# Weight tiles for field-pair products: a ring of three tiles loaded twelve pairs ahead, in place of two tiles loaded six pairs ahead

## The chip, the cores and the metric

The kernel runs on one core of one Trainium2 chip. The core has a tensor engine (PE; its weight loads are listed as PEld), a vector engine (DVE), a scalar engine (ACT), a GpSimd engine (POOL), a sync engine (SP) and 16 DMA engines that move data between HBM and the on-chip memory SBUF. The metric is the device time of one execution in microseconds (us). Before the change the median of six runs is 760.24 us (759.88 to 760.63).

## The reference

There are 32 fields. The input `r_inputs` has, for each of 1024 rows of the batch, one vector of 128 numbers per field. `W` holds one 128 by 128 matrix for each of the 496 pairs of fields i < j. For every pair the vector of field i is multiplied by the pair's matrix, and the result is multiplied element by element with the vector of field j:

```python
v_i = inputs[:, I_IDX, :]
v_j = inputs[:, J_IDX, :]
transformed = jnp.einsum('bpd,ped->bpe', v_i, W)
return transformed * v_j
```

All numbers are float32. The output has 1024 x 496 x 128 numbers, 260 MB; the weights are 32.5 MB and the fields 16.8 MB. The profile counts 49.28 MB read from HBM and 260.05 MB written.

## The kernel before

**Order of the pairs.** `_pairs()` walks i from 30 down to 0 and, for each i, j from i+1 to 31. Row i thus has 31-i pairs; the rows grow longer, and field 0, as the last i, is needed only for the last 31 pairs (465 to 495). It is never a j. A pair is done in two halves of 512 rows of the batch; the loop variable `u` counts halves and `q = u // 2` counts pairs. The batch lies along the free dimension, so a field is a tile of 128 partitions by 1024 numbers (4 KB in a partition, 512 KB in all).

**Loads.** `load_x(f)` loads one field, from SP before the loop and from ACT's queue inside it: at the first pair of row i it loads field i-7. Each field has a tile of its own that stays for the whole kernel (pool `x`). `load_w(c)` loads a weight tile: the matrices of eight pairs (`WL = 8`), 4 KB in a partition, 512 KB. Weight tiles come from a ring of `WB` = 2 buffers (pool `wr`). The first two are loaded before the loop by SP; the dictionary `w_at` says at which pair the others are issued, on ACT's queue (line 194): tile c at pair 8c-11, or later where the tile that held the buffer is still read by matmuls on unsplit weights (tile 2 at pair 8, tile 3 at pair 16).

**Splitting.** The first five rows (15 pairs, `nq0`) are multiplied as they are (line 159). For all others float32 is split into two shorter parts, and a product takes three matmuls. `split_w(c)` splits the weights of two pairs: ACT makes `wh` (line 95), POOL makes `wl` and `wd` (lines 96 to 98). It is taken from the list `todo` from pair 2c-5 on, so the first split of weight tile c comes six pairs after the tile's load was issued. `split_x(f, a)` does the same for half a field (lines 110 to 112, and `xd` on POOL at line 116 or, for the first ten split fields, on DVE at line 203). One item of `todo` is taken per pair.

**A half pair.** `first(u)` issues the matmuls of `wh` and `wl` (line 162), and ACT scales their sum in PSUM (line 163). `second(u)`, three halves later, adds the matmul of `wd` (line 171), and DVE multiplies PSUM by field j into the output tile `ot` (line 177). Three pairs share an `ot` of 1.5 MB, and SP writes it out when it is full (line 184); the first group and the last four pairs go out in smaller pieces. There are four `ot` buffers, so DVE can begin a group only when the write of the group four before it has landed.

**What sets the order.** The schedule is the program's order (`tc.manual_schedule()`): on each engine instructions run in the order in which the loop issues them, and a waiting instruction holds up all that is behind it on its engine. ACT's queue thus carries the issues of weight and field loads, the `wh` and `xh` splits and the scaling of every half pair; POOL's carries the rest of the splits; SP's carries the writes. A DMA is also issued only after the earlier DMA on the same completion semaphore has landed.

Of the kernel before, what the change touches and what calls it, by code (L numbers as in the profile page):

```python
# [7 lines left out]
F32 = mybir.dt.float32  # L8
# [3 lines left out]
P = 128  # L12
NF = 32
NQ = NF * (NF - 1) // 2
BT = 1024
HB = 512
WC = 2
WL = 8
# [3 lines left out]
SHARED = 10  # L22
XDLAG = 10
LAG = 3
WB = 2
WLEAD = 6
XLEAD = 5


# [6 lines left out]
def kernel(  # L36
# [22 lines left out]
    nc = tc.nc  # L59
# [3 lines left out]
    xpool = ctx.enter_context(tc.tile_pool(name="x", bufs=1))  # L63
    spool = ctx.enter_context(tc.tile_pool(name="xs", bufs=2))
    rpool = ctx.enter_context(tc.tile_pool(name="wr", bufs=WB))
    wpool = ctx.enter_context(tc.tile_pool(name="ws", bufs=4))
# [4 lines left out]

    def load_x(f, n=1, pieces=1, eng=None):

        t = xpool.tile([P, n, BT], F32, tag=f"x{f}", name=f"x_{f}")
        s = BT // pieces
        for k in range(pieces):
            (eng or nc.sync).dma_start(out=t[:, :, k * s : (k + 1) * s], in_=xt[:, f : f + n, k * s : (k + 1) * s])
        for k in range(n):
            x_sb[f + k] = t[:, k, :]
# [3 lines left out]
    def load_w(c, splits=(0, WL), eng=nc.scalar):  # L83
        w_raw[c] = rpool.tile([P, WL, P], F32, tag="w", name=f"w_{c}")
        for a, b in zip(splits, splits[1:]):
            eng.dma_start(out=w_raw[c][:, a:b, :], in_=wt[c, :, a:b, :])
# [44 lines left out]

    load_w(0, (0, 1, WL), nc.sync)
    load_x(NF - 2, pieces=2, eng=nc.scalar)
    load_x(NF - 1, pieces=2, eng=nc.scalar)
    load_x(NF - 3)
    load_x(NF - 4)
    load_w(1, eng=nc.sync)
    for f in range(NF - 5, NF - 4 - XLEAD, -1):
        load_x(f)


    w_at = {}
    for c in range(WB, -(-NQ // WL)):
        free = (c - WB + 1) * WL if (c - WB) * WL < nq0 else 0
        w_at[max(c * WL - 3 * WC + 1 - WLEAD, free)] = c


    ctx.enter_context(tc.manual_schedule())
# [3 lines left out]
    def first(u):  # L152
        q, h = divmod(u, 2)
        i, c = pairs[q][0], q // WC
        r = slice(q % WC * P, (q % WC + 1) * P)
        s = slice(h * HB, (h + 1) * HB)
        po[u] = ppool.tile([P, HB], F32, tag="po", name=f"po_{u}")
        if q < nq0:
            nc.tensor.matmul(po[u], w_raw[q // WL][:, q % WL, :], x_sb[i][:, s], start=True, stop=True)  # L159
        else:  # L160
            for t in (0, 1):
                nc.tensor.matmul(po[u], w_s[c][t][:, r], x_s[i][t][:, s], start=t == 0, stop=t == 1)  # L162
            nc.scalar.mul(po[u], po[u], 1.0 + EPS)  # L163

    def second(u):
        q, h = divmod(u, 2)
        i, j = pairs[q]
        r = slice(q % WC * P, (q % WC + 1) * P)
        s = slice(h * HB, (h + 1) * HB)
        if q >= nq0:  # L170
            nc.tensor.matmul(  # L171
                po[u], w_s[q // WC][2][:, r], x_s[i][2][:, s], start=False, stop=True, skip_group_check=True
            )
        g, k = divmod(q, OG)
        if k == 0 and h == 0:
            ots[g] = opool.tile([P, OG, BT], F32, tag="ot", name=f"ot_{g}")
        nc.vector.tensor_tensor(ots[g][:, k, s], po.pop(u), x_sb[j][:, s], ALU.mult)  # L177
        if q >= NQ - 2:
            nc.sync.dma_start(out=out[g, :, k, s], in_=ots[g][:, k, s])
        elif g == 0 or q >= NQ - 1 - OG:  # L180
            if h == 1:
                nc.sync.dma_start(out=out[g, :, k], in_=ots[g][:, k])
        elif k == OG - 1 and h == 1:
            nc.sync.dma_start(out=out[g], in_=ots[g])

    for u in range(2 * NQ + LAG):
        q = u // 2
        if u < 2 * NQ:
            i, j = pairs[q]
            if u % 2 == 0 and j == i + 1 and 0 <= i - 2 - XLEAD:  # L190
                load_x(i - 2 - XLEAD, eng=nc.scalar)
            first(u)
            if u % 2 == 1 and q in w_at:
                load_w(w_at[q])
        if u >= LAG:
            second(u - LAG)
        if u % 2 == 1:
            ready = [t for t in todo if t[0] <= q]
            if ready:
                ready[0][2](u)  # L200
                todo.remove(ready[0])
        while later and later[0][0] <= u:
            nc.vector.tensor_tensor(*later.pop(0)[1:], ALU.subtract)  # L203
# [28 lines left out]
```

## Time and profile before

The profiled execution took 759.89 us by its own time, 0.35 us under the median of the six runs; its span, from the first to the last instruction, is 758.0 us, so 1.89 us lie around it.

| | busy us | share of the span |
|---|---|---|
| PE matmul | 707.4 | 93% |
| DVE | 629.1 | 83% |
| ACT | 625.4 | 83% |
| POOL | 597.0 | 79% |
| DMA, 310.07 MB in 758 us | mean 409 GB/s | |

| transfer | count | size KB | median us from issue to landing |
|---|---|---|---|
| `ot` to HBM | 163 | 1536 | 13.5 |
| weight tile, from ACT | 60 | 512 | 9.0 |
| field, from ACT | 24 | 512 | 9.0 |
| field, from SP | 6 | 512 | 8.5 |

Busy time is a union of intervals, and matmuls overlap, so PE's 93% is not 93% of what PE could do. In the tables of stretches each row has a time window in us, the busy time of each engine with the count of its instructions, the granted clock of PE, the mean share of time in which the 16 DMA engines had a packet, and the rate. A DMA engine's packets overlap by some nanoseconds, so a share of 1.00 to 1.02 means that all 16 were occupied. In lists of waits a row reads: engine and line that waited, what it waited for, the sum in us, how often, the longest.

### The profile page before, as it was taken

The page shows a single profiled execution, that of the slowest core. Times are in us where ns is not written, and L with a number is a line of the kernel's source. Part 1 is how long each engine was busy: PE and PEld are TensorE (multiplying, and loading weights), DVE is VectorE, ACT ScalarE, POOL GpSimd, SP SyncE. Part 2 cuts the span into 40 slices and gives each one's busy share as a digit, 9 for nine tenths or more (in the row PEclk, how much of TensorE's full clock was granted, in tenths as well). Part 3 has the DMA queues.
Part 4 walks back from the last instruction along what each step waited for, and adds up shares of the span by engine and source line. Part 5 has one row for each costly group of instructions (what it writes and reads, how often), then busy time and mean ns, then how long its engine had stood idle before and what let it go on. Part 6 is the DMA issues. An engine that isn't in the chain of part 4 may idle for free.

```text
span 758.0 us, 11264 instructions
## 1 busy us (share of the span) xinstructions
PE 707.4 (93%) x2946; PEld 549.5 (72%) x2946; DVE 629.1 (83%) x1012; ACT 625.4 (83%) x1256; POOL 597.0 (79%) x863
## 2 busy tenths in 40 slices
PE   7979999999999999999998999999999999999992
PEld 3557778777777777777787777778787777777771
DVE  4869989997888879788797888888888888888883
ACT  1368889988888888888887978889899898989881
POOL 0959999999888987977878787888887878786650
PEclk9999999999999999999999999999999999999996
DMA  9999999999999999999999999999999999999996
GB/s 349 426 409 380 425 414 421 424 426 425 424 425 422 426 422 399 424 418 407 407 404 423 414 420 417 396 419 410 409 412 410 409 420 406 403 417 415 419 407 256
DMA packets 38800, 310.07 MB, mean 409 GB/s; under 512 B 4304, under 2 KB 4432, under 8 KB 17872
## 3 DMA queue, kind: packets, MB, share of 16 engines
q1 hardware_dynamic: 26064, 264.25, 83.2%
q10 hardware_dynamic: 12672, 45.09, 16.0%
q8 instruction: 24, 0.39, 0.2%
q14 instruction: 40, 0.33, 0.1%
HBM read 49.28 MB, written 260.05 MB: 408 GB/s over the span
## 4 chain that ended last, share of the span: by engine, by line
DMA 53%; PE 20%; DVE 19%; POOL 3%; issue 2%; ACT 1%; DVEq 0%; ACTq 0%; SPq 0%; POOLq 0%
DMA out_dram<-ot 50%; DVE ot L177 18%; PE po L162 13%; PE po L171 7%; DMA x<-in_xt_dram 2%; POOL xl L111 1%; DMA w<-in_wt_dram 1%; DVE xd L203 1%; POOL xl L112 1%; POOL xd L116 1%; POOL wl L96 0%; POOL wd L98 0%; ACT po L163 0%; DVEq L177 0%; POOL wd L97 0%
## 5 line engine op out<-in xcount | busy, mean ns | idle before, releaser
L177 DVE TENSOR_TENSOR ot<-po,x 128x512 f32<-128x512 f32 x992 | 614.9, 682 | 113.3 <-DMA out_dram<-ot 46.4
L163 ACT ACTIVATE po<-po 128x512 f32<-128x512 f32 x962 | 540.4, 582 | 58.6 <-PE po L162 23.0
L162 PE MATMUL po<-xh,wh 128*128 128x512 f32 x962 | 381.8, 397 | 12.8 <-DVE ot L177 11.9
L171 PE MATMUL po<-xd,wd 128*128 128x512 f32 x962 | 377.1, 392 | 13.7 <-ACT po L163 11.4
L162 PE MATMUL po<-xl,wl 128*128 128x512 f32 x962 | 378.2, 393 | 5.4 <-POOL wl L96 5.3
L96 POOL TENSOR_TENSOR wl<-w,wh 128x256 fp32r<-128x256 f32 x241 | 182.3, 756 | 74.1 <-ACT wh L95 63.6
L162 PEld LDWEIGHTS po<-xh,wh 128*128 128x128 f32 x962 | 181.2, 188 | 70.9 <-DVE ot L177 33.0
L171 PEld LDWEIGHTS po<-xd,wd 128*128 128x128 f32 x962 | 181.3, 188 | 56.5 <-issue 6.3
L162 PEld LDWEIGHTS po<-xl,wl 128*128 128x128 f32 x962 | 181.4, 189 | 46.2 <-POOL wl L96 10.2
L98 POOL TENSOR_TENSOR wd<-wl,wd 128x256 fp32r<-128x256 f32 x241 | 179.2, 743 | 20.1
L95 ACT ACTIVATE wh<-w 128x256 fp32r<-128x256 f32 x241 | 99.8, 414 | 42.1 <-DMA w<-in_wt_dram 36.6
L97 POOL TENSOR_SCALAR wd<-wh 128x256 fp32r<-128x256 f32 x241 | 98.8, 410 | 20.3
L111 POOL TENSOR_TENSOR xl<-x,xh 128x512 fp32r<-128x512 f32 x52 | 69.3, 1333 | 18.5 <-ACT xh L110 18.0
L116 POOL TENSOR_TENSOR xd<-xh,xl 128x512 fp32r<-128x512 f32 x32 | 41.4, 1292 | 2.7
L110 ACT ACTIVATE xh<-x 128x512 fp32r<-128x512 f32 x52 | 32.5, 629 | 12.6 <-DMA x<-in_xt_dram 12.6
L112 POOL TENSOR_SCALAR xl<-xl 128x512 fp32r<-128x512 f32 x52 | 33.3, 641 | 4.6
L159 PE MATMUL po<-x,w 128*128 128x512 f32 x60 | 28.4, 636 | 4.4 <-DMA x<-in_xt_dram 4.4
L159 PEld LDWEIGHTS po<-x,w 128*128 128x128 f32 x60 | 11.8, 202 | 20.2 <-issue 13.0
L203 DVE TENSOR_TENSOR xd<-xh,xl 128x512 fp32r<-128x512 f32 x20 | 17.1, 854 | 3.6 <-POOL xl L112 3.6
L110 ACT ACT_TABLE_LOAD x1 | 1.3, 1283 | 4.5 <-DMA w<-in_wt_dram 4.5
L219 POOL MEMSET const-float32-0.0<- 128x1 f32 x1 | 0.1, 99 | 0.2 <-issue 0.2
L219 POOL MEMSET const-bfloat16-1.0<- 128x1 bf16 x1 | 0.1, 102 | 0.0
(2 smaller groups left out, 0.2 us busy)
## 6 DMA issues: line engine op xcount, KB each, us to landing
out_dram<-ot SPq DMA_DIRECT2D x163, 1536.0 KB, 13.5
w<-in_wt_dram ACTq DMA_DIRECT2D x60, 512.0 KB, 9.0
x<-in_xt_dram ACTq DMA_DIRECT2D x24, 512.0 KB, 9.0
x<-in_xt_dram SPq DMA_DIRECT2D x6, 512.0 KB, 8.5
out_dram<-ot SPq DMA_DIRECT2D x5, 512.0 KB, 10.8
x<-in_xt_dram ACTq DMA_DIRECT2D x4, 256.0 KB, 5.8
out_dram<-ot SPq DMA_DIRECT2D x4, 256.0 KB, 10.1
w<-in_wt_dram SPq DMA_DIRECT2D x1, 512.0 KB, 8.1
```

Of the source, the lines that this page charges most:

```text
L95: nc.scalar.mul(h, raw, 1.0 - 2.0**-13)
L96: nc.gpsimd.tensor_tensor(l, raw, h.bitcast(F32), ALU.subtract)
L97: nc.gpsimd.tensor_scalar(d, h.bitcast(F32), EPS, 1.0, ALU.mult, ALU.mult)
L98: nc.gpsimd.tensor_tensor(d, l.bitcast(F32), d.bitcast(F32), ALU.subtract)
L111: nc.gpsimd.tensor_tensor(l, x_sb[f][:, s], h.bitcast(F32), ALU.subtract)
L112: nc.gpsimd.tensor_scalar(l, l.bitcast(F32), 1.0 / EPS, 1.0, ALU.mult, ALU.mult)
L116: nc.gpsimd.tensor_tensor(d, h.bitcast(F32), l.bitcast(F32), ALU.subtract)
L159: nc.tensor.matmul(po[u], w_raw[q // WL][:, q % WL, :], x_sb[i][:, s], start=True, stop=True)
L162: nc.tensor.matmul(po[u], w_s[c][t][:, r], x_s[i][t][:, s], start=t == 0, stop=t == 1)
L163: nc.scalar.mul(po[u], po[u], 1.0 + EPS)
L171: nc.tensor.matmul(po[u], w_s[q // WC][2][:, r], x_s[i][2][:, s], start=False, stop=True, skip_group_check=True)
L177: nc.vector.tensor_tensor(ots[g][:, k, s], po.pop(u), x_sb[j][:, s], ALU.mult)
```

## The change

The ring of weight tiles gets a third buffer (`WB` 2 to 3), and a weight tile is issued six pairs earlier (8c-17 in place of 8c-11). The third tile, number 2, is loaded by SP before the loop; in the loop, tile 3 is issued at pair 8, where tile 2 was, and tile 4 at pair 16, where tile 3 was. SBUF's room for the third buffer comes from field 0, which loses its own tile: it passes through the ring of weight tiles, between tiles 54 and 55, loaded on ACT's queue at pair 421 in place of pair 276. The three weight tiles after it (55 to 57) keep the old distance of six pairs. On PE, DVE and POOL the instructions stay in the same order; ACT has one load fewer and SP one more, ahead of its first write.

```diff
-WB = 2
-WLEAD = 6
+WB = 3
+WLEAD = 12
+XAFTER = 54
 ...
     def load_x(f, n=1, pieces=1, eng=None):
-        t = xpool.tile([P, n, BT], F32, tag=f"x{f}", name=f"x_{f}")
+        if f == 0:
+            t = rpool.tile([P, WL, P], F32, tag="w", name="x_0").rearrange("p q e -> p (q e)").unsqueeze(1)
+        else:
+            t = xpool.tile([P, n, BT], F32, tag=f"x{f}", name=f"x_{f}")
 ...
     for f in range(NF - 5, NF - 4 - XLEAD, -1):
         load_x(f)
+    load_w(2, eng=nc.sync)
 ...
         free = (c - WB + 1) * WL if (c - WB) * WL < nq0 else 0
-        w_at[max(c * WL - 3 * WC + 1 - WLEAD, free)] = c
+        early = 0 if XAFTER < c <= XAFTER + WB else WLEAD - 6
+        w_at[max(c * WL - 3 * WC - 5 - early, free)] = c
+    x_at = XAFTER * WL - 11
+    assert x_at not in w_at and len(w_at) == NQ // WL - WB
 ...
-            if u % 2 == 0 and j == i + 1 and 0 <= i - 2 - XLEAD:
+            if u % 2 == 0 and j == i + 1 and 0 < i - 2 - XLEAD:
                 load_x(i - 2 - XLEAD, eng=nc.scalar)
             first(u)
             if u % 2 == 1 and q in w_at:
                 load_w(w_at[q])
+            if u == 2 * x_at + 1:
+                load_x(0, eng=nc.scalar)
```

## The prediction

> **What bounds the kernel now.** I read the page first, then the stretches, then the waits.
>
> ```profile
> DMA  9999999999999999999999999999999999999996
> GB/s 349 426 409 380 425 414 421 424 426 425 424 425 422 426 422 399 424 418 407 407 404 423 414 420 417 396 419 410 409 412 410 409 420 406 403 417 415 419 407 256
> DMA 53%; PE 20%; DVE 19%; POOL 3%; issue 2%; ACT 1%; DVEq 0%; ACTq 0%; SPq 0%; POOLq 0%
> ```
>
> The DMA engines are occupied from the second slice to the last but one, and the chain that ended last lies on DMA for 53%, nearly all of it writes. So a wait on an engine costs time only where it leaves the DMA engines short of issued work. The rates fall below 426 GB/s in two places: the fourth slice (about 57 to 76 us), and many slices from the sixteenth on. The stretches and the waits tell the two apart.
>
> ```profile
> 20.00:40.00 20.00, 20.00 (x63) 11.60 (x62) 17.48 (x29) 7.64 (x17) 17.45 (x22) 1.00 1.02 426
> 40.00:60.00 20.00, 14.85 (x58) 11.48 (x56) 13.45 (x21) 13.77 (x29) 12.86 (x19) 0.91 0.98 399
> 60.00:80.00 20.00, 18.70 (x81) 15.17 (x82) 19.89 (x31) 17.57 (x37) 18.49 (x25) 1.00 1.00 395
> 80.00:100.00 20.00, 18.11 (x72) 13.70 (x71) 18.39 (x29) 15.81 (x33) 18.49 (x25) 0.94 1.01 427
> 100.00:120.00 20.00, 20.00 (x87) 16.48 (x86) 19.37 (x31) 18.49 (x39) 18.41 (x28) 0.97 1.01 409
> 300.00:745.00 445.00, 427.61 (x1829) 339.48 (x1827) 375.76 (x614) 391.58 (x782) 349.98 (x516) 1.00 1.00 412
> ```
>
> DVE's waits before 140 us, and then its waits after:
>
> ```profile
> DVE ot L177 <- PE po L171: 8.7, 7, 5.0
> ...
> DVE ot L177 <- DMA out_dram<-ot: 46.4, 51, 1.4
> DVE ot L177 <- PE po L171: 25.3, 32, 1.7
> ```
>
> After 140 us DVE waits 51 times for a write to land: all four `ot` buffers are in use, so DMA has all the work it can be given, and the 412 GB/s of 300 to 745 us is its own pace. Before 140 us DVE never waits for a write: there the engines set the pace, and the low 399 and 395 are shortage. What sets the end is seen in the tail:
>
> ```profile
> 745.00:751.00 6.00, 0.00 (x0) 0.00 (x0) 0.98 (x2) 0.00 (x0) 0.00 (x0) 0.60 0.95 374
> 751.00:757.00 6.00, 0.00 (x0) 0.00 (x0) 0.00 (x0) 0.00 (x0) 0.00 (x0) 0.50 0.07 29
> ```
>
> A share of 0.07 is about one engine of sixteen: I read it as one DMA engine that is some 6 us behind the others and finishes alone. If so, the end is set by that engine's own work, and the write landings that release `ot` are its landings.
>
> Now the waits that the change touches, in 30 to 50 us, and rows of POOL and of ACT from the order in time:
>
> ```profile
> ACT wh L95 <- DMA w<-in_wt_dram: 14.9, 2, 9.1
> POOL wl L96 <- ACT wh L95: 7.0, 3, 6.4
> DVE ot L177 <- PE po L171: 6.2, 3, 5.0
> ...
> 45.63 0.72 POOL L96 TENSOR_TENSOR wl<-w,wh 128x256 fp32r<-128x256 f32 x1 [6.36 <-ACT wh L95]
> ...
> 20.82 0.34 ACTq L86 DMA_DIRECT2D w<-in_wt_dram  x1
> 34.74 0.33 ACTq L86 DMA_DIRECT2D w<-in_wt_dram  x1
> 45.14 0.42 ACT L95 ACTIVATE wh<-w 128x256 fp32r<-128x256 f32 x1 [5.80 <-DMA w<-in_wt_dram]
> ```
>
> Tile 2 is issued at 20.82 and awaited by ACT until 30.68 (9.07 us); tile 3 is issued at 34.74 and awaited until 45.14 (5.80 us). The first costs little, since PE is still in the unsplit rows until 32.2. The second stops the engines: POOL idles 6.36, PE and DVE about 5 us.
>
> **The change part by part.**
>
> *Tiles 2 to 4 at the start.* Tile 2 now goes out on SP behind four fields; the landing row of such loads (8.5 us) puts it in SBUF by about 20 us, before ACT's `wh` at 21. Tile 3 takes the place of 20.82 and lands near 31; POOL wants it at 39.3, when its split of tile 2 ends. Tile 4 takes that of 34.74 and lands near 45; four chunks of 2.0 us (0.76 + 0.41 + 0.74 and gaps) and a field's two halves of 1.9 us later POOL wants it, at 39.3 + 8 + 3.8 = 51. So the stop at 39 to 45 goes, and what is late next is POOL itself (18.49 busy of 20, the same number in many stretches: full) and DVE (19.89). The engines are 5 to 6 us earlier from 45 us on and keep that until they meet the write landings, now at 147.9 us in the chain, then sooner.
>
> *What of it reaches the end.* Not 5 us, since DMA was occupied in part. The shortage is (426 - 399)/426 x 20 = 1.27 us in 40 to 60 and (426 - 395)/426 x 20 = 1.46 us in 60 to 80, together 2.7; with 100 to 120 (0.8 us) 3.5 us for the mean DMA engine. For the engine that ends last less of it is shortage: over its whole run, some 2.2 to 756.6 us, it moves its share of 310.07 MB, as 411 GB/s for all sixteen, so against 411 the same stretches lack 0.58 + 0.78 = 1.4 us, and 100 to 120 lacks 0.1. Bounds: 1.4 to 3.5; I take 2.0, nearer the lower, since the end goes by the last engine. That the shortage is refilled follows from the rate of work: between the writes issued at 48.72 and 89.47 us SP and ACT issued nine writes and six loads (the trace's issue times); at 1536 KB and 512 KB and 426 GB/s this is 9 x 3.69 + 6 x 1.23 = 40.6 us of DMA in 40.75 us. The engines keep DMA just filled if they do not start from an empty queue.
>
> *Later weight waits.* After 130 us ACT still waits 18.8 us for weight tiles (31 times, longest 2.9). With twelve pairs, some 17.8 us at (744.7 - 32.2)/481 = 1.48 us a pair, against a landing of 9.0 (at most 12.1), they vanish, except for tiles 55 to 57. I cost this at nothing: the writes already issued hide it (DVE waits 46.4 us for landings in the same stretch). If that cover were gone, up to 18.8 us would count.
>
> *Does the earlier load wait for its buffer?* At pair 8c-17 the tile three before has been read in full: PE's pair 8c-17 itself uses its last `wl`. So no wait of ACT is added, and the scaling behind the issue on ACT is not held. Zero; at worst a POOL chunk of 2 us, hidden by the landings.
>
> *SP's extra load.* It waits for an earlier load's completion, and the first write is behind it. A wait of this kind held SP 2.0 us before the first write already. Between zero and one landing (8.5 us) the first writes are later; 20 to 40 us shows a share of 1.02, so DMA has other work. The load adds no byte. Zero, with 0.3 us as the upper end (its issue).
>
> *Field 0.* Loaded 145 pairs later, same bytes, DMA occupied at both places: zero. It needs the buffer of tile 52 at pair 421, whose last split is taken at 417: four pairs, what the ring had before. Its own split is taken from pair 436 on, 15 pairs or 22 us after, so it has landed. Tile 57 takes its buffer at 445. Zero, at worst one wait of the size seen (2.9 us), hidden.
>
> The Trainium skill's DMA: Bandwidth & Descriptors, section Issuing engines are not separate DMA queues, says that transfers from all issuing engines share the same 16 DMA engines and interleave. It speaks against the change: by it an earlier load only displaces a write, and the sum would be 0; the rows of 40 to 80 us, where DMA was short of work, make it 2.0. The same page, section Latency and other measured facts, says that engines 7 and 15 are usually slower than the rest; the tail's 0.07 agrees with one such engine, though no view here names it.
>
> Sum: 758.0 - 2.0 = 756.0 us of span, with 1.89 around it 757.9 for this execution, or 760.24 - 2.0 = 758.2 against the median.
>
> **The rivals.**
>
> *No change* (0.25). The engine that ends last was never short, because it was behind and had a backlog while the others ran dry. For it: the tail's 6 us, and that the late weight waits of 18.8 us visibly cost nothing. Against it: in 20 to 40 us the loads and writes run at 426 with all engines occupied, so little can have built up by 50 us. Time 760.24 - 0.2 = 760.0.
>
> *The whole stop counts* (0.05). If the last engine was idle as long as PE, 5.4 us of the 5.8 reach the end: 754.8. Against it: the share of 0.98 in 40 to 60.
>
> *Slower: the ring at field 0 stops ACT* (0.10). Field 0, four pairs after the last split of tile 52 is due, waits for a late POOL (busy 14 to 18 of 20 us there), and the scaling behind it on ACT waits too. A stop of ACT counts only beyond what is already issued: the last engine's 6 us. It needs a stop of 6 us to start, and one of 10 us, as long as the worst wait in this trace (9.1) and one more pair, would give 760.24 + 4 = 764.2. For it: three tiles in a row keep the short distance behind field 0. Against it: the longest late wait was 2.9 us.
>
> **How the numbers follow.** About 0.2%, 1.5 us, is what a measurement of this kernel can tell from no change: 758.7 to 761.8. The main case (0.60) spans 1.4 to 3.5 us of gain; 0.5 of it falls under 758.7 and 0.1 above. With the 0.05 of the full stop that makes faster 0.55. Same: 0.1 of the main case and 0.22 of the rival, 0.32. Slower: 0.10 and 0.03 of scatter in the rival, 0.13. The range goes from 755.6 (somewhat beyond the 3.5) to 760.9, which takes in the rival of no change and leaves out the slower one and the full stop.
>
> **What would show it.** Right: no wait of ACT for a weight tile at 45 us, POOL without the 6.4 us hole, 40 to 80 us at 415 GB/s or more, DVE's first wait for a landing well before 147 us, the tail unchanged with a lone engine for 6 us. Wrong: a rate in 40 to 80 us that rises while the end stays (the rival of no change); ACT waiting near pair 421 to 451, at some 640 to 690 us; or a rate after 300 us that moves from 412, since I hold DMA's own pace there fixed, and 1% of it is 4 us.

## The result and the profile after

The changed kernel took 758.15 us (median of 19 runs, 757.68 to 761.24), beside 760.63 us of the kernel before on the same chips (41 runs, 758.88 to 763.85). The ratio is 0.9967, with a 95% interval of 0.9959 to 0.9974: some 2.5 us faster, where 2.0 were forecast. The profiled execution of the changed kernel took 756.1 us of span, 1.9 us less than the one before.

From the page of the changed kernel, the DMA share and rate in 40 slices, and the chain that ended last:

```profile
DMA  9999999999999999999999999999999999999996
GB/s 353 426 424 429 426 425 427 427 422 421 407 417 411 428 408 417 421 407 415 418 414 407 407 423 401 409 416 401 405 421 408 419 413 411 412 408 421 419 404 258
DMA 59%; DVE 21%; PE 15%; POOL 2%; issue 1%; DVEq 0%; ACT 0%; ACTq 0%; SPq 0%; POOLq 0%
```

The dip of the fourth slice (380 GB/s before) has gone. From the sixteenth slice on the rates go up and down as they did before. The slices from the eleventh to the fifteenth, 422 to 426 GB/s before, are lower now (407 to 428). The same in stretches (columns as before: window, engines, granted clock, DMA share, GB/s):

```profile
40.00:60.00 20.00, 18.31 (x81) 14.61 (x80) 18.98 (x29) 17.45 (x37) 17.78 (x25) 1.00 1.01 425
60.00:80.00 20.00, 18.42 (x79) 14.14 (x77) 17.34 (x28) 17.47 (x37) 18.40 (x26) 1.00 1.01 426
80.00:100.00 20.00, 18.91 (x82) 15.23 (x82) 18.25 (x31) 18.09 (x38) 18.49 (x26) 1.00 1.01 428
100.00:120.00 20.00, 18.34 (x75) 13.55 (x75) 16.50 (x28) 16.72 (x34) 18.49 (x26) 1.00 1.01 425
140.00:300.00 160.00, 151.83 (x635) 116.51 (x634) 131.70 (x216) 138.25 (x276) 136.10 (x195) 1.00 1.01 417
300.00:745.00 445.00, 428.50 (x1826) 338.64 (x1824) 376.44 (x614) 393.72 (x781) 348.87 (x516) 1.00 1.00 412
```

The 399 and 395 GB/s of 40 to 80 us are now 425 and 426, the 409 of 100 to 120 is 425, and 300 to 745 us is 412 in both. One row goes the other way: 140 to 300 us runs at 417 now, where the kernel before has

```profile
140.00:300.00 160.00, 152.51 (x646) 118.83 (x645) 134.78 (x218) 139.11 (x282) 141.19 (x202) 1.00 1.01 424
```

The two engines that stood still in the kernel before, in the changed kernel's order of time:

```profile
39.22 0.74 POOL L101 TENSOR_TENSOR wl<-w,wh 128x256 fp32r<-128x256 f32 x1 [0.63 <-ACT wh L100]
...
20.32 0.33 ACTq L91 DMA_DIRECT2D w<-in_wt_dram  x1
21.62 0.42 ACT L100 ACTIVATE wh<-w 128x256 fp32r<-128x256 f32 x1 [0.50 <-issue]
38.74 0.41 ACT L100 ACTIVATE wh<-w 128x256 fp32r<-128x256 f32 x1
```

ACT splits tile 2 at 21.62 us and tile 3 at 38.74 without a wait for a load (9.07 and 5.80 us before), and POOL's hole shrinks from 6.36 to 0.63 us. DVE's waits up to 140 us, and from the chain that ended last, in order of time, its first wait for a landing:

```profile
DVE ot L186 <- DMA out_dram<-ot: 6.1, 7, 1.4
...
38.81 13.25 DMA out_dram<-ot
52.80 0.68 DVE ot L186
```

DVE meets a full set of output buffers at 52 us, in place of 160, and 7 times before 140 us, where it never did before. So DMA has all the work it can take from then on (425 to 428 GB/s up to 120 us). The tail has the same form as before:

```profile
745.00:751.00 6.00, 0.00 (x0) 0.00 (x0) 0.00 (x0) 0.00 (x0) 0.00 (x0) 0.54 0.68 265
751.00:757.00 6.00, 0.00 (x0) 0.00 (x0) 0.00 (x0) 0.00 (x0) 0.00 (x0) 0.50 0.04 16
```

The other fifteen engines finish some 2 us earlier, and one goes on alone. The completion records of both traces say the same more sharply: the last write's sixteenth completion comes 5.8 us after the median one in both kernels, at 756.96 us before and at 755.04 now.

These records show more. Each transfer has sixteen of them, read here as one from each DMA engine, so the time from the eighth to the sixteenth is how far the last engine is behind. Its median over the transfers of a stretch, in us:

| kernel | 60 to 80 us | 140 to 180 | 180 to 220 | 300 to 360 | 580 to 660 |
|---|---|---|---|---|---|
| before | 0.6 | 2.0 | 4.1 | 6.0 | 6.3 |
| changed | 1.9 | 5.5 | 6.0 | 6.2 | 6.1 |

At 60 to 80 us of the kernel before the last engine had almost no backlog, so what is lost there is lost to it too; the rival of no change had it behind by then. Later it falls some 6 us behind and stays there, and it gets there sooner in the changed kernel. The stretches in which the backlog still grows are those of 424 to 428 GB/s, those in which it stands at 6 us are those of 412 to 417.

The packet records show what the low rates of 40 to 80 us were made of. Against 426 GB/s the kernel before lost some 2.9 us there: 0.8 us in which engines had no packet, and 2.1 us because packets took longer (6.6% of the 12 KB packets took 550 ns or more, 0.4% in the changed kernel). By the mean, 2.7 transfers were issued and not yet landed, and 5.1 in the changed kernel. So the shortage is one of transfers under way more than of idle engines; why packets take longer with few of them was not followed.

### The profile page after: what moved, and what is told of

The parts are those of the page before. It is cut to its first block, busy times and chain, and to the rows that moved or that the text cites. A ratio compares the mean times of both kernels' runs of the same rounds, so it can differ in the third digit from the quotient of the medians.

```text
span 756.1 us, 11322 instructions
## 1 busy us (share of the span) xinstructions
PE 709.5 (94%) x2946; PEld 546.0 (72%) x2946; DVE 623.6 (82%) x1012; ACT 630.9 (83%) x1256; POOL 595.2 (79%) x863
## 4 chain that ended last, share of the span: by engine, by line
DMA 59%; DVE 21%; PE 15%; POOL 2%; issue 1%; DVEq 0%; ACT 0%; ACTq 0%; SPq 0%; POOLq 0%
DMA out_dram<-ot 57%; DVE ot L186 20%; PE po L171 10%; PE po L180 5%; DMA x<-in_xt_dram 2%; POOL xl L116 1%; DVE xd L214 1%; POOL xl L117 0%; POOL wl L101 0%; DVEq L186 0%; ACT po L172 0%; POOL xd L121 0%; ACTq L82 0%; POOL wd L103 0%; ACT xh L115 0%
## 5 line engine op out<-in xcount | busy, mean ns | idle before, releaser
L172 ACT ACTIVATE po<-po 128x512 f32<-128x512 f32 x962 | 548.6, 583 | 92.2 <-PE po L171 39.9
L101 POOL TENSOR_TENSOR wl<-w,wh 128x256 fp32r<-128x256 f32 x241 | 179.7, 746 | 74.4 <-ACT wh L100 71.3
L103 POOL TENSOR_TENSOR wd<-wl,wd 128x256 fp32r<-128x256 f32 x241 | 181.5, 753 | 20.1
L214 DVE TENSOR_TENSOR xd<-xh,xl 128x512 fp32r<-128x512 f32 x20 | 15.3, 764 | 3.8 <-POOL xl L117 3.8
## 6 DMA issues: line engine op xcount, KB each, us to landing
out_dram<-ot SPq DMA_DIRECT2D x4, 256.0 KB, 10.1
```

Of the source, the lines that this page charges most:

```text
L101: nc.gpsimd.tensor_tensor(l, raw, h.bitcast(F32), ALU.subtract)
L103: nc.gpsimd.tensor_tensor(d, l.bitcast(F32), d.bitcast(F32), ALU.subtract)
```

## The experiments

Eight kernels were run first, in two groups of four, each group on one chip; then four more on a third. All are compared with runs of the kernel before on the same chip, whose medians were 761.04, 760.80 and 760.58 us. A ratio and its interval come from all the runs and need not equal the quotient of the two medians. Diffs are against the changed kernel unless the text says otherwise.

### Which part carries the gain

**The start alone.** Tiles 2 to 4 early as in the change, everything after at six pairs.

```diff
-        early = 0 if XAFTER < c <= XAFTER + WB else WLEAD - 6
+        early = WLEAD - 6 if c < 5 else 0
 ...
-    x_at = XAFTER * WL - 11
+    x_at = XAFTER * WL - 10
```

> The ring of three with tiles 2 to 4 early as in the changed kernel, all later tiles six pairs ahead as before, field 0 through the ring. Theory (the gain is the shortage of DMA work at 40 to 80 us alone): ratio 0.997, some 2 us faster than before, with 40 to 80 us at 425 GB/s and the late waits of ACT for weight tiles back at 15 us or more. Rival (the twelve pairs after the start carry part of it): less than half of the gain, ratio 0.9985 or more.

Measured: 759.22 us (12 runs), ratio 0.9984, interval 0.9971 to 0.9997. The stretches of its profile, and ACT's wait for weight tiles in 80 to 106 us:

```profile
40.00:60.00 20.00, 19.46 (x85) 15.57 (x84) 19.95 (x31) 18.56 (x39) 17.33 (x24) 1.00 1.01 425
60.00:80.00 20.00, 16.86 (x72) 13.02 (x71) 19.17 (x28) 13.86 (x29) 18.35 (x25) 1.00 1.01 427
80.00:100.00 20.00, 18.59 (x73) 14.91 (x74) 17.20 (x27) 17.55 (x37) 17.29 (x26) 0.91 0.99 399
...
ACT wh L100 <- DMA w<-in_wt_dram: 4.6, 2, 3.5
```

The shortage of 40 to 80 us is gone and ACT's late waits are back (14.6 us) as expected, but with six pairs a stop of 3.5 us comes some 40 us later, at 77 to 80 us (the kernel before has one of 2.9 us at 92 to 95), and DMA runs short behind it: 399 GB/s in 80 to 100. The early tiles alone give about half of the gain by the ratio (1.2 us) and nearly three quarters by the medians (1.8 us). The expected 0.997 lies just outside the interval.

**The distance alone.** Twelve pairs from tile 5 on, tiles 2 to 4 where the kernel before has them.

```diff
-    load_w(2, eng=nc.sync)
 ...
-    for c in range(WB, -(-NQ // WL)):
-        free = (c - WB + 1) * WL if (c - WB) * WL < nq0 else 0
+    for c in range(2, -(-NQ // WL)):
+        free = {2: 8, 3: 16, 4: 21}.get(c, 0)
 ...
```

> The ring of three with twelve pairs from tile 5 on and field 0 through the ring, but tiles 2, 3 and 4 issued on ACT's queue at pairs 8, 16 and 21 as before. Theory: ratio 1.000 (0.9985 to 1.0015), POOL's hole of about 6 us at 39 to 45 us is back, 40 to 80 us under 405 GB/s, and no late wait of ACT for weights. Rival (the late tiles carry the gain): ratio 0.997 to 0.998.

Measured: 759.50 us (12 runs), ratio 0.9982, interval 0.9972 to 0.9992. POOL's hole is back (6.5 us), as expected, but the ratio and the rates are not those expected: 40 to 80 us ran at 414 and 410 GB/s. A likely part of the reason stands in the program's order: tile 5 is now issued at pair 23 in place of 29 (at 50.45 us, 58.97 before), right behind tile 4 and the stop, so a load that the kernel before issued later can fill a part of the shortage. No run tests this by itself.

**Tile 2 early, tiles 3 and 4 not.**

```diff
-        free = (c - WB + 1) * WL if (c - WB) * WL < nq0 else 0
+        free = {3: 16, 4: 21}.get(c, 0)
```

> The changed kernel with tile 2 loaded by SP before the loop, but tiles 3 and 4 issued at pairs 16 and 21 as before. Theory: the wait for tile 2 (9.07 us on ACT) was hidden by the unsplit rows and that for tile 3 (5.80 us) was the stop, so the stop of about 6 us stays and the ratio is 1.000 (0.9985 to 1.0015). Rival (tile 2's early arrival is what counts): ratio 0.997, with 40 to 80 us at 415 GB/s or more.

Measured: 759.02 us (12 runs), ratio 0.9978, interval 0.9965 to 0.9991, with ACT's wait for tile 3 still there (5.5 us) and 426 and 408 GB/s in 40 to 80 us. The expected 1.000 is outside the interval. This kernel also has the twelve pairs from tile 5 on, which the expectation had left out of account; it can't be told from the one before it, so what tile 2 gives by itself stays open.

**Split at tile 13.** The three runs fit a theory with a wider stretch: what counts is how far DMA gets in the first 130 us, and both the early tiles and the distance of tiles 5 to 12 serve that. Two more kernels cut at tile 12, which is issued at pair 79. The first has the change up to there and six pairs after:

```diff
-        early = 0 if XAFTER < c <= XAFTER + WB else WLEAD - 6
+        early = WLEAD - 6 if c <= 12 else 0
 ...
-    x_at = XAFTER * WL - 11
+    x_at = XAFTER * WL - 10
```

The second loads weights as the kernel before up to there and twelve pairs ahead after; it has the diff of the distance alone and this:

```diff
-        early = 0 if XAFTER < c <= XAFTER + WB else WLEAD - 6
+        early = 0 if c <= 12 or XAFTER < c <= XAFTER + WB else WLEAD - 6
```

> The changed kernel with twelve pairs up to weight tile 12 alone (issued by pair 79, some 130 us) and six pairs after it. Theory, amended by the first runs (the gain is the shortage of DMA work up to some 130 us, and tiles 5 to 12 need the twelve pairs as well, since with six a stop of 3.5 us came at 82 us): as the changed kernel, ratio within 0.0007 of it, 0 to 130 us at 415 GB/s or more. Rival (the later tiles, with ACT's late waits of 15 to 19 us, carry half of the gain): ratio 0.998 to 0.9985.

> The opposite: tiles 2 to 4 issued where the kernel before has them, six pairs up to tile 12, twelve pairs from tile 13 on, field 0 through the ring. Theory: ratio 1.000 (0.9988 to 1.0012), 0 to 130 us at 402 to 404 GB/s, though ACT's late waits for weights are gone. Rival: ratio 0.998 to 0.9985.

> The changed kernel itself, beside the next three on one chip. Ratio to before 0.996 to 0.9975, with 0 to 130 us at 416 GB/s in its profile.

Measured beside each other: the changed kernel 758.22 us (5 runs), ratio 0.9960 (0.9947 to 0.9973), with 415 GB/s in the first 130 us of this profile; twelve pairs up to tile 12, 758.92 us (12 runs), ratio 0.9992 (0.9972 to 1.0012); twelve pairs from tile 13, 760.45 us (12 runs), ratio 0.9997 (0.9985 to 1.0009). The first 130 us and the rest, for the kernel before, the changed one, and the two halves:

```profile
0.00:130.00 130.00, 117.27 (x431) 82.98 (x432) 107.57 (x165) 85.12 (x174) 96.58 (x133) 0.97 0.99 403
130.00:745.00 615.00, 590.12 (x2517) 466.54 (x2515) 520.54 (x847) 540.26 (x1084) 500.41 (x731) 1.00 1.01 415
```
```profile
0.00:130.00 130.00, 119.61 (x447) 83.15 (x448) 107.05 (x170) 89.68 (x181) 101.88 (x141) 1.00 1.00 416
130.00:745.00 615.00, 589.94 (x2501) 462.80 (x2499) 516.58 (x843) 541.20 (x1075) 493.35 (x723) 1.00 1.00 414
```
```profile
0.00:130.00 130.00, 119.69 (x447) 83.21 (x448) 107.40 (x170) 89.58 (x181) 101.71 (x141) 1.00 1.00 415
130.00:745.00 615.00, 588.07 (x2501) 463.55 (x2499) 516.89 (x843) 539.26 (x1075) 493.02 (x723) 1.00 1.00 413
```
```profile
0.00:130.00 130.00, 117.49 (x432) 83.01 (x433) 107.29 (x166) 85.17 (x174) 96.70 (x133) 0.97 0.99 404
130.00:745.00 615.00, 592.39 (x2515) 465.77 (x2513) 520.07 (x847) 543.18 (x1083) 498.27 (x731) 1.00 1.01 415
```

ACT's waits for weight tiles after 130 us, in the kernel before and in the second of the two:

```profile
ACT wh L95 <- DMA w<-in_wt_dram: 18.8, 31, 2.9
```
```profile
ACT wh L100 <- DMA w<-in_wt_dram: 4.2, 4, 2.0
```

The second half of the change is worth nothing that can be measured: twelve pairs for the 46 tiles from 13 on, field 0 in the ring included, cut ACT's waits for weights after 130 us from 18.8 to 4.2 us and leave the time where it was (the interval allows 1.1 us of gain or 0.7 of loss). The first half is less clean. Its profile shows the whole effect (415 GB/s), and its median has 1.7 of the changed kernel's 2.4 us on that chip, but four of its twelve runs lie at 761.6 to 765.7 us, and its interval takes in both no gain and the full gain. That 0.7 us between it and the changed kernel belong to the late tiles is possible and not shown.

Put together, the rate of the first 130 us and the median against the kernel before on the same chip:

| kernel | GB/s, 0 to 130 us | us against before | ratio |
|---|---|---|---|
| changed | 416 | -2.5 | 0.9967 |
| twelve pairs to tile 12 | 415 | -1.7 | 0.9992, wide |
| tile 2 early, twelve from tile 5 | 411 | -2.0 | 0.9978 |
| start alone | 410 | -1.8 | 0.9984 |
| twelve from tile 5 | 409 | -1.5 | 0.9982 |
| twelve from tile 13 | 404 | -0.1 | 0.9997 |
| before, field 0 late | 402 | -0.4 | 0.9999 |

The rows of the four that are not shown above, in the order of the table (tile 2, start alone, from tile 5, field 0 late):

```profile
0.00:130.00 130.00, 116.96 (x437) 83.28 (x438) 110.04 (x168) 87.36 (x177) 97.31 (x135) 0.99 1.00 411
0.00:130.00 130.00, 120.14 (x447) 85.27 (x448) 111.50 (x170) 87.56 (x181) 99.17 (x138) 0.99 1.00 410
0.00:130.00 130.00, 116.45 (x432) 81.90 (x433) 109.20 (x166) 86.53 (x175) 96.57 (x133) 0.99 1.00 409
0.00:130.00 130.00, 116.13 (x429) 82.02 (x430) 107.36 (x165) 84.85 (x174) 95.79 (x132) 0.97 0.99 402
```

The rate after 130 us is 413 to 415 in all of them. So the early part tells kernels with a gain from those without. Each rate is that of one profiled execution, up to 1.6 us from its kernel's median. The first 130 us repeat well all the same: the kernel before and the two that load weights as it does up to there (field 0 late, twelve from tile 13) gave 402 to 404. Single stretches of 20 us repeat less well: the same three had from 377 to 406 in 40 to 60 us.

Whether the two ways to fill the early part overlap is not shown. By the rates they add: 410 and 409 are 7 and 6 above 403, and the whole change is 13 above. By the ratios they add too (0.0016 and 0.0018, against 0.0033). By the medians, 1.8 and 1.5 us against 2.5, they would overlap somewhat. The intervals are too wide to decide.

**Field 0 late,** in the kernel before:

```diff
-            if u % 2 == 0 and j == i + 1 and 0 <= i - 2 - XLEAD:
+            if u % 2 == 0 and j == i + 1 and 0 < i - 2 - XLEAD:
 ...
                 load_w(w_at[q])
+            if u == 843:
+                load_x(0, eng=nc.scalar)
```

> The kernel before, with field 0 in its own tile but loaded at pair 421 in place of 276. Theory (the same bytes at another place of a stretch in which DMA has all the work it can take): ratio 1.000 (0.9985 to 1.0015). Rival (moving the load frees DMA while writes are awaited, or crowds the end): 1.2 us, the DMA time of 512 KB, either way, ratio 0.9984 or 1.0016.

Measured: 760.60 us (12 runs), ratio 0.9999, interval 0.9988 to 1.0010. Nothing, as expected.

### What a late stop costs

Tile 30, and in a second kernel tiles 30 to 32, are issued one pair before their first split.

```diff
-        w_at[max(c * WL - 3 * WC - 5 - early, free)] = c
+        w_at[c * WL - 6 if c in (30,) else max(c * WL - 3 * WC - 5 - early, free)] = c
```

> The changed kernel with weight tile 30 issued one pair before its first split in place of twelve pairs, at some 350 us, so that ACT stops for about 8 to 10 us in the stretch where DVE waits for writes to land. Theory (a stop of the engines counts only beyond the work that is already issued, some 6 to 11 us there): 0 to 2 us slower than the changed kernel, ratio to before 0.997 to 1.000. Rival (the engines set the pace there): the whole stop, 8 to 10 us, ratio 1.008 to 1.011.

> The same with tiles 30, 31 and 32, three stops of 8 to 10 us some 12 us apart. Theory: the first is covered, but the engines are only some 5% faster than DMA there and win back under 1 us between two stops, so the second and third count nearly in full: 10 to 20 us slower than the changed kernel, ratio 1.010 to 1.023. Rival (whatever stop of this size is covered again and again): under 3 us, ratio under 1.001. Rival (engines set the pace): 24 to 30 us, ratio 1.029 or more.

ACT's waits for weight tiles in the first (355 to 400 us), then in the second (355 to 430 us):

```profile
ACT wh L100 <- DMA w<-in_wt_dram: 13.1, 1, 13.1
```
```profile
ACT wh L100 <- DMA w<-in_wt_dram: 17.3, 3, 6.6
```

One stop of 13.1 us: 764.03 us (9 runs), ratio 1.0043 (1.0028 to 1.0058), against the changed kernel's 0.9967 a loss of 0.0076 or 5.8 us. The stop came out longer than planned; 13.1 - 5.8 = 7.3 us of it were covered, within the 6 to 11 us of issued work that the expectation named, though above its 0 to 2 us of loss for a shorter stop. Three stops: 772.79 us (4 runs), ratio 1.0142 (1.0112 to 1.0172), a loss of 0.0175 or 13.3 us, in the range of the first theory. The 17.3 us of stops are those of the profiled execution, the fastest of the four: 768.21 us, 10.1 above the changed kernel's median, so 7.2 us of them were covered, as much as of the single stop. The stops of the other three are not on record.

The completion records tell what covers a stop. The time from the eighth to the sixteenth, as above:

| kernel | 300 to 360 us | 380 to 400 | 440 to 480 | 580 to 660 |
|---|---|---|---|---|
| changed | 6.2 | 7.4 | 7.0 | 6.1 |
| one stop | 6.3 | 0.2 | 2.7 | 5.0 |
| three stops | 6.1 | 0.3 | 1.9 | 4.5 |

The stop uses up the backlog of the engine that is behind, and the backlog takes more than 200 us to come back. So a stop is covered once, by work already issued, and the cover is not won back between stops some 12 us apart.

### Whether bytes alone set the late time

The changed kernel without four of its late weight loads; the pairs of those tiles use the weights of the tile before.

```diff
-                load_w(w_at[q])
+                if w_at[q] in (30, 33, 36, 39):
+                    w_raw[w_at[q]] = w_raw[w_at[q] - 1]
+                else:
+                    load_w(w_at[q])
```

> The changed kernel without the loads of weight tiles 30, 33, 36 and 39; their pairs are multiplied with the weights of the tile before, so those outputs are others. 2 MB less for DMA between 340 and 500 us, no engine instruction less but four load issues. Theory (after 50 us the DMA engine that ends last is never short of work, so time goes by bytes): 4 x 1.27 = 5.1 us less than the changed kernel, at 411 GB/s, ratio to before 0.990. Rival (engines or the depth of the output buffers set the pace late): under 1.5 us less, ratio 0.995 to 0.997.

Measured: 755.15 us (4 runs), ratio 0.9923 (0.9903 to 0.9943), against 0.9967 a gain of 3.3 us, about two thirds of the 5.1. Neither expectation holds in full. Its chain and the stretch from which loads were taken:

```profile
PE 45%; DMA 39%; DVE 11%; POOL 3%; issue 1%; ACT 0%; DVEq 0%; SPq 0%; ACTq 0%; POOLq 0%
...
340.00:500.00 160.00, 155.06 (x673) 125.22 (x672) 141.81 (x226) 144.31 (x290) 133.39 (x196) 1.00 1.00 408
```

The chain, 59% on DMA and 15% on PE in the changed kernel, is 39% and 45% here, and the rate falls to 408. That fits engines that are only a little faster than DMA, so that less DMA work soon leaves the engines as the limit; how the missing third divides was not followed further.

### A version below both

Fields 23 to 2 are loaded two at a time, 8 KB in a partition in place of 4.

```diff
-            if u % 2 == 0 and j == i + 1 and 0 < i - 2 - XLEAD:
-                load_x(i - 2 - XLEAD, eng=nc.scalar)
+            f = i - 2 - XLEAD
+            if u % 2 == 0 and j == i + 1 and 0 < f and (f == 1 or f % 2 == 1):
+                load_x(max(f - 1, 1), n=1 if f == 1 else 2, eng=nc.scalar)
```

> The changed kernel with fields 23 to 2 loaded two at a time (1 MB, 8 KB in a partition) at the row of the first, so 11 loads in place of 22. Theory (time goes by the work of the DMA engine that ends last; loads in 4 KB pieces moved at 372 GB/s by their queue's share, writes in 12 KB pieces at 419): 11.5 MB at a rate between the two saves 0.5 to 2 us against the changed kernel, ratio to before 0.994 to 0.996. Rival (the piece's size does not matter, the lower rate comes from reading): no gain, ratio 0.997.

> The fields loaded two at a time, as before, now beside the changed kernel on one chip. Theory (less work for the DMA engines by larger pieces): 0.5 to 1 us under the changed kernel. Rival (the difference of 0.0016 in the first comparison was the chip): within 0.4 us of it.

Measured: 757.47 us (7 runs, six of them within 0.3 us and one at 763.76), ratio 0.9951 (0.9934 to 0.9968); and beside the changed kernel 757.54 us (5 runs), ratio 0.9948 (0.9936 to 0.9960). In that second comparison its five runs (756.97 to 757.64) all lie under the changed kernel's five (757.90 to 759.32), 0.7 us by the medians, within the 0.5 to 1 expected. That the larger pieces are the reason was argued, not shown: the loads of every second field also start a row earlier than they did.

## Why the prediction was right, and where it was not

- *The bound.* Right for this change. Waits of the engines count only where DMA runs short of issued work: with ACT's late waits gone (from 18.8 to 4.2 us, tile 13 on) the time did not move, and the made stop counted only beyond some 7 us. The rate after 300 us stayed at 412, which the prediction had asked for. What it called shortage was for the larger part longer packets, not idle engines (2.1 us of 2.9). DMA's lead is narrow, though: with 2 MB less to move PE leads the chain.
- *Tiles 2 to 4.* Right in each sign that it named: no wait at 21 and 39 us, POOL's hole gone, 40 to 80 us at 425 instead of "415 GB/s or more", the engines ahead until they meet the landings, at 52 us. (The 147.9 us that it gives for the kernel before is the start of the write; DVE waited for its landing, at 160.) The sentence that they keep their lead from there was right for the whole change and wrong for the early tiles alone: with six pairs a second stop comes at 77 to 80 us. The twelve pairs of tiles 5 to 12 are what keeps the lead, and the prediction priced the later tiles only after 130 us, at nothing. Without the early tiles, twelve pairs from tile 5 on gave 1.4 us by the ratio, from tile 13 on 0.2.
- *What reaches the end.* 2.0 us taken between 1.4 and 3.5; 2.5 by the medians, 1.9 by the two profiles. The choice of less than the mean engine's shortage held: that engine was 13 GB/s short over 130 us, 13/416 x 130 = 4.1 us, and only 45 to 60% came out at the end. The rest is given back mostly in the stretch of 140 to 300 us, where 424 GB/s became 417: the last engine's backlog is full sooner there (5.5 us at 140 to 180, 2.0 before), and the others then wait sooner for its landings. The prediction had no such row; the narrower price for the last engine stood in for it. That the number came so near is in part luck: the tiles that it priced gave 1.2 to 1.8 us by themselves, and the rest came with later tiles, which it put at nothing.
- *The late waits, the ring at field 0, SP's extra load.* At nothing, and so it was: ratio 0.9997 for the late half with the ring at field 0, 0.9999 for field 0 alone; ACT's wait for weights is 0.5 us in 638 to 700 us. SP's first write went out at 11.43 us, 11.50 before.
- *The cover.* The rival that is slower needed a stop beyond the "6 us" of the last engine. A made stop of 13.1 us showed a cover of 7.3, and a backlog of 6.3 that was gone after it.
- *The lone engine.* The tail has it again, 5.8 us behind. The made stops show that its backlog is what covers a stop, as it must if this engine sets the end; no run here moved work away from it.

## What to carry to other kernels

Before pricing a wait, find where the transfer engines lack issued work: the waits for the first tiles cost 1.2 to 1.8 us here, while some 15 us of waits later cost nothing that could be measured, because DMA already had issued work to do. Measure the shortage in the rate of the stretch against the full rate beside it, and don't expect all of it at the end if one engine is slower than the rest. And undo the parts of a change one at a time: here two early parts gave about half each, and a third, which took most of the waiting away, gave nothing.

## What was not expected of the hardware

One of the 16 DMA engines lags the others by about 6 us (at most 8.9) in the later part of both traces; of the other fifteen the last is 1.6 us behind, by the median of the transfers from 300 to 740 us. The packet records of both traces have runs of 12 KB packets that follow each other without a gap at 475 to 480 ns a packet, where 460 is the usual number. The records name no engine, so that these runs are the lagging engine's is a reading; an estimate agrees with it: 16 x 12288 bytes in 478 ns are 411 GB/s, beside the 412 of 300 to 745 us. In the profiles of the single stop and of the second measurement of the changed kernel a second engine is as late at the end (5.0 and 4.0 us). The Trainium skill's DMA: Bandwidth & Descriptors, section Latency and other measured facts, says that engines 7 and 15 are usually slower, and its guess at the cause is tied to transfers issued by GpSimd. The slow engine fits, but here all loads and writes were issued by SP and ACT. At the very end, when the engine works alone, its 4 KB and 2 KB packets take 159 and 84 ns, the usual numbers. So in these two traces it was slow only while the rest were busy.
